# Two attention layers on one core: position rows in order of use, held weights, and the work at the seams of the second attention

## The chip, the core and the metric

The kernel runs on one core of one Trainium2 chip. The metric is the device time of one execution in microseconds. TensorE (PE) does the matmuls, VectorE (DVE), ScalarE (ACT) and GpSimd (POOL) work on what it leaves, and SyncE (SP) issues nearly all DMAs. All data are 32-bit floats.

## The reference

`x` has 8 batches of 32 x 32 positions (1024 tokens) and 512 channels. Each of two layers adds attention over the group-normalised input to its input:

```python
# layer 0: 16 heads of 32 channels
q, k, v = split(gn(x) @ w_qkv);  x = x + softmax(q * 32**-0.5 @ k.T) @ v @ w_proj + b_proj
# layer 1: 4 heads of 128 channels, with relative position logits
q = gn(x) @ Wq * 128**-0.5;  k = gn(x) @ Wk;  v = gn(x) @ Wv
scores = q @ k.T + rel_w[..., None, :] + rel_h[..., :, None]   # from q with pos_emb_w, pos_emb_h
x = x + softmax(scores) @ v @ Wo
```

## The kernel before

The batches are pipelined. In pass `b` of the outer loop, `attention_0` of batch `b` gives the beat, and `side_by_side` interleaves with it, by costs that each piece yields, the rest: the output projection WP of batch `b-1` (`after_0`), the output projection WO of batch `b-2` (`after_1`), the projections WQ1, WK1, WV1 of batch `b-1` (`second`), its `attention_1`, and the first projections of batch `b+1` (`before_0`). `total` is the expected sum of the costs (`PRODUCT` = 28 for one 512 x 512 projection, `SECOND` for `second`); the rest may advance while `done * steps < total * at`, with 65 steps. The steps of `attention_1` cost nothing, except in pass 7, so its 64 steps run as one block between two steps of `attention_0`. In pass 7 its first 32 steps are interleaved with `attention_0` of batch 7. Pass 8 has no `attention_0`, and after it `after_last` does the last WO projection. Below, batches are numbered 0 to 7, and "the opening of batch 2" is the start of its `attention_1`.

A projection is done with seven products of half-size blocks in place of eight, for each of two units (`seven`; `two_first` and `five_alone` in the last projection). A product takes one weight factor from `Stream`, and each product calls `stream.ahead()`, which loads the factor used seven products later. A factor of WV1 is two DMAs, kept for both units; the others are one. `forming` makes the four sums of the other operand that the seven products need (four DVE instructions, line L392). `woven(main, side, start, gap, places)` lets a side piece advance at certain steps of a main piece.

The second attention adds position logits to the scores. `position_logits` computes a short tile `pp` with matmuls and copies it to `pos` (L837, ACT) in four rounds, woven between the products of WK1 and WV1, each round followed by three yields. `Seeds` then writes `pos` to DRAM in two broadcast forms per head, `pc` and `pr` (L859), and reads back, in the 64 steps of the attention (4 heads, 2 halves of queries, 8 blocks of keys), one `columns` tile per 8 steps (L877) and one row tile per step (L880) into a ring of 8 in `pos`. POOL adds columns to rows (`add_up`, L887), and ACT copies the sum into a PSUM bank (`put`, L895). The score matmul accumulates onto that bank (L936), ACT takes exp (L938), the product with v is L949, and DVE adds up the exps (L963, L965). The copy of step `i` makes its ring slot free for the row of step `i+8`. At step `i`, copies are made up to step `i + AHEAD - 1` behind its exp; the four banks are those that `attention_0` used for its scores. `finish` ends each group of 8 steps: the sum is transposed and reduced on DVE (L688, L689), folded by a small matmul (L982), and the result divides q's columns on DVE (L703 to L720).

The order within each engine's queue is that of a planner, which runs through the program with its own costs and may put an instruction that is ready ahead of an earlier one that is not. `tc.issue_after(ins)` keeps the instructions of a block behind `ins` in its engine's queue.

Of the kernel before, what the change touches and what calls it, by code (L numbers as in the profile page):

```python
# [27 lines left out]
def quick_path(  # L28
# [23 lines left out]
    nc = tc.nc  # L52
# [4 lines left out]
    NT = N // P  # L57
# [136 lines left out]
    class Stream:  # L194
# [3 lines left out]
        def __init__(self, plan):  # L198
            self.plan = plan
            self.tiles = {}  # L200
            self.at = -1
            self.uses = iter([(n, i) for n, (_, _, _, some) in enumerate(plan) for i in some])
            for _ in ORDER:
                self.ahead()

        def load(self, n, i):
            m, rows, u, some = self.plan[n]
            if rows and u == 1 and not m.kept:
# [26 lines left out]

        def ahead(self):
            use = next(self.uses, None)
            if use is not None:
                self.load(*use)


# [298 lines left out]
    def in_two_parts(  # L540
        x, m, sinks, name, room=None, done=lambda u: None, behind=None, in_turn=False
    ):
# [32 lines left out]
        begin, rest = (3, five_alone) if in_turn else (2, five_last)  # L575
        yield from woven(products(), (next(sums) for _ in range(begin)), 0, 1)
        for u in range(2):
# [231 lines left out]
    def position_logits(q, turned, pos, b):  # L809
# [6 lines left out]
        for t in range(IW // (2 * G)):  # L816
# [24 lines left out]
            yield -2  # L841
            yield 0
            yield 0

    class Seeds:
# [4 lines left out]
        def __init__(self, pos, b):  # L850
            self.pos, self.b = pos, b
            self.kept = []
            for h in range(H1):
# [9 lines left out]
            self.rows, self.columns, self.summed = {}, {}, 0  # L863
            for i in range(self.ROWS):
                self.load(i)

        def load(self, i):
# [5 lines left out]
            if j == 0:  # L873
                to = self.columns[group] = mem.tile(
                    [P, NB], F32, tag="columns", name=f"columns_{self.b}_{group}", bufs=2
                )
                nc.sync.dma_start(to, by_columns)  # L877
            at = i % self.ROWS
            to = self.rows[i] = self.pos[:, at // NH, (at % NH) * NB : (at % NH + 1) * NB]
            nc.sync.dma_start(  # L880
                to, by_rows[16 * j : 16 * j + 16].unsqueeze(1).to_broadcast([16, P // 16, NB])
            )

        def add_up(self, upto):
# [13 lines left out]

    def attention_1(q, k, v, seeds, b, beside=0):

        steps = [(h, c, j) for h in range(H1) for c in range(NH) for j in range(NT)]
        state = {}
        AHEAD = 4
        scored = [None]
# [83 lines left out]
        for i, at in enumerate(steps):  # L988
# [13 lines left out]
            if i + 1 < beside:  # L1002
                prepare(i + 1)
            yield 0
        back(*pending)
        yield 0
        run(finish(*state.pop("ended")))
        state["pool"].__exit__(None, None, None)
# [166 lines left out]
    def second(b, st):  # L1175
# [19 lines left out]
        def queries(u):  # L1195
# [7 lines left out]
        keys_and_values = chain(  # L1203
            project_T(fs, WK1, k, f"k1_{b}"), project_rows(fs, WV1, v, f"v1_{b}")
        )
# [53 lines left out]
    def after_last(b, st):  # L1259
# [3 lines left out]
        sinks = [Onto(halves(xT, u), then=put_out(b, st, xT, u)) for u in range(2)]  # L1263
        run(in_two_parts(x, WO, sinks, f"wo_{b}", behind=(None, None, None, lambda: begun[0]), in_turn=True))

# [47 lines left out]
    PRODUCT = 2 * len(ORDER) * HC  # L1313
    SECOND = 3 * PRODUCT - 8

# [23 lines left out]

    states = [{} for _ in range(B)]  # L1340
    load_first(states[0])
    WV0.add_up([nc.gpsimd] * 2 + [nc.vector] * 2, nc.gpsimd, keep=True)
# [13 lines left out]

    def at_once(do):
        do()
        return
        yield  # L1360

    run(woven(before_first(states[0]), key_sums(), 3, 1))
    for b in range(B + 1):
# [5 lines left out]
        def forms_0(b=b, st=here):  # L1369
            st["ao0"] = forms(st["q0"], f"ao0_{b}")  # L1370

        def forms_past(b=b, st=past):
            forms_1(b - 2, st)

        if last is not None:
# [9 lines left out]
            else:  # L1385
                norm = norm_1(b - 1, last, after=lambda: summed[0], behind=lambda: begun[0])
            first = after_0(b - 1, last, forms_past if past is not None else None)
            rest.append(first if past is not None else with_norm(first))
            total += PRODUCT
# [3 lines left out]
            else:  # L1393
# [5 lines left out]
            attention = later(  # L1399
                lambda st, steps: attention_1(*st.pop("at"), steps), last, H1 * NT if shared else 0  # L1400
            )
# [520 lines left out]
```

## Time and profile before

| | |
|---|---|
| time, median of 3 runs | 3735.8 us (3732.56 to 3737.66) |
| profiled execution: time, span | 3736.12 us, 3734.3 us |
| mean granted TensorE clock | 0.992 |
| TensorE busy | 3659.2 us (98%) |
| DVE, ACT, POOL busy | 2562.3, 2032.8, 1300.5 us |
| DMA moved | 419.40 MB, mean 112 GB/s |
| row loads pos<-pr (L880) | 512 of 256 KB, median 4.3 us to landing |

The profile is of one execution. A line of a timeline gives start, length, engine, line of the program, operation, output and input, a count of merged instructions, and in brackets the idle time before it and what ended it. A line of the chain of waits gives who waited for whom, the sum, the number of times and the longest. SPq is SP's queue of DMA issues.

### The profile page before, as it was taken

To read this page: it belongs to the slowest core of one execution; us is meant where nothing else is said; L and a number is where in the kernel's file an instruction comes from. 1 tells how busy PE (TensorE), PEld (TensorE's weight loads), DVE (VectorE), ACT (ScalarE), POOL (GpSimd) and SP (SyncE) were. 2 spreads that over 40 slices of the span, in tenths; PEclk is the share of its full clock that TensorE was granted. 3 is DMA by queue.
4 is the path that set the end of the run, shared out by engine and by line. 5 is a ranking of instruction groups with operands and counts; after the bars stand their busy time and mean duration, and the time that the engine had idled before them with its cause. 6 is when DMAs were issued, how large, how long until landed. Compare 5 with 4: busy or idle time off the path is not lost.

```text
span 3734.3 us, 81210 instructions
## 1 busy us (share of the span) xinstructions
PE 3659.2 (98%) x33992; PEld 1251.2 (34%) x33998; DVE 2562.3 (69%) x2905; ACT 2032.8 (54%) x2281; POOL 1300.5 (35%) x847
## 2 busy tenths in 40 slices
PE   9999999999999999999999999999999999999998
PEld 4232243322433234332343323433234332333343
DVE  6778667685676856669576685766857668566545
ACT  3555655446554465544665446654566545655353
POOL 1342155131541315413163131721327112165254
PEclk9999999999999999999999999999999999999999
DMA  6122183233733337333372344713447133433385
GB/s 190 63 94 81 43 190 124 67 105 68 189 120 93 83 81 191 101 96 92 90 198 75 95 96 107 195 58 100 90 106 215 42 97 78 106 115 122 97 206 131
DMA packets 575158, 419.40 MB, mean 112 GB/s; under 512 B 279840, under 2 KB 471616, under 8 KB 573760
## 3 DMA queue, kind: packets, MB, share of 16 engines
q1 hardware_dynamic: 563152, 398.33, 39.9%
q0 software_dynamic: 2608, 13.70, 1.0%
q8 instruction: 270, 4.42, 0.5%
q10 hardware_dynamic: 9024, 2.10, 0.3%
q14 instruction: 104, 0.85, 0.1%
HBM read 321.72 MB, written 92.27 MB: 111 GB/s over the span
## 4 chain that ended last, share of the span: by engine, by line
PE 83%; DVE 7%; POOL 2%; ACT 2%; issue 2%; DMA 1%; SPq 1%; DVEq 0%; POOLq 0%; ACTq 0%
PE ps L739 13%; PE acc L765 11%; PE ps L936 11%; PE acc L949 11%; PE y_q L353 4%; PE y_v L353 4%; PE y_k L353 4%; PE z_q L353 3%; PE x_v L353 3%; PE z_v L353 3%; PE x_k L353 3%; DVE e_room L777 3%; PE z_k L353 2%; PE x_q L353 2%; PE y_wp L353 2%
## 5 line engine op out<-in xcount | busy, mean ns | idle before, releaser
L777 DVE TENSOR_TENSOR e_room<-e_room 128x2048 f32<-128x2048 f32 x448 | 1087.6, 2428 | 487.6 <-ACT e_room L754 485.7
L754 ACT ACTIVATE e_room<-ps 128x2048 f32<-128x2048 f32 x512 | 961.8, 1879 | 752.3 <-PE ps L739 717.4
L887 POOL TENSOR_TENSOR pos<-pos,columns 128x512 f32<-128x512 f32 x512 | 738.0, 1472 | 240.9 <-DMA pos<-pr 240.1
L739 PE MATMUL ps<-q,k 32*64 32x512 f32 x8192 | 592.6, 613 | 1.1 <-ACT e_room L754 1.0
L949 PE MATMUL acc<-e,v 128*128 128x512 f32 x1024 | 533.6, 605 | 27.6 <-ACT e L938 27.6
L765 PE MATMUL acc<-e_room,v 128*32 128x512 f32 x4096 | 551.1, 604 | 5.2 <-ACT e_room L754 5.2
L936 PE MATMUL ps<-q,k 128*128 128x512 f32 x1024 | 538.1, 610 | 9.5 <-ACT ps L895 9.5
L938 ACT ACTIVATE e<-ps 128x512 f32<-128x512 f32 x512 | 304.9, 597 | 261.9 <-PE ps L936 247.3
L965 DVE TENSOR_TENSOR es<-es,e 128x512 f32<-128x512 f32 x384 | 276.7, 721 | 155.8 <-ACT e L938 150.2
L895 ACT COPY ps<-pos 128x512 f32<-128x512 f32 x512 | 298.2, 590 | 92.3 <-POOL pos L887 49.7
L720 POOL TENSOR_TENSOR q<-q,su 128x512 f32<-128x512 f32 x64 | 94.8, 1481 | 568.0 <-DVE su L716 545.6
L949 PEld LDWEIGHTS acc<-e,v 128*128 128x128 f32 x1024 | 195.9, 193 | 283.2 <-issue 219.0
L936 PEld LDWEIGHTS ps<-q,k 128*128 128x128 f32 x1024 | 191.6, 194 | 248.6 <-issue 216.6
L739 PEld LDWEIGHTS ps<-q,k 32*64 32x64 f32 x8192 | 122.9, 129 | 395.6 <-issue 220.8
L765 PEld LDWEIGHTS acc<-e_room,v 128*32 128x32 f32 x4096 | 82.0, 108 | 420.6 <-issue 363.6
L605 POOL TENSOR_TENSOR k<-b_k,p_k 128x512 f32<-128x512 f32 x32 | 55.0, 1719 | 472.2 <-ACT p_k L457 461.5
L605 POOL TENSOR_TENSOR q<-b_q,p_q 128x512 f32<-128x512 f32 x32 | 67.3, 2102 | 356.9 <-ACT p_q L457 356.8
L605 POOL TENSOR_TENSOR v<-b_v,p_v 128x512 f32<-128x512 f32 x32 | 55.5, 1734 | 317.5 <-ACT p_v L457 306.2
L837 ACT COPY pos<-pp 32x512 f32<-32x512 f32 x128 | 104.1, 814 | 32.0 <-PE pp L828 30.8
L963 DVE TENSOR_TENSOR es<-e,e 128x512 f32<-128x512 f32 x64 | 66.2, 1035 | 56.2 <-ACT e L938 56.1
L681 DVE STREAM_TRANSPOSE tu<-su 128x512 f32<-128x512 f32 x64 | 45.2, 706 | 76.9 <-ACT su L679 76.7
L353 PE MATMUL y_q<-f_xn,w_q 128*32 128x512 f32 x768 | 91.4, 593 | 1.3 <-DVE a_q L443 0.6
(225 smaller groups left out, 4452.7 us busy)
## 6 DMA issues: line engine op xcount, KB each, us to landing
pos<-pr SPq DMA_DIRECT2D x512, 256.0 KB, 4.3
w_qkv<-ws_qkv SPq DMA_DIRECT2D x168, 128.0 KB, 2.6
d<-x0T SPq DMA_DIRECT2D x32, 512.0 KB, 5.8
x1T<-d SPq DMA_DIRECT2D x32, 512.0 KB, 5.4
d<-x1T SPq DMA_DIRECT2D x32, 512.0 KB, 3.5
pc<-pos SPq DMA_DIRECT2D x32, 512.0 KB, 8.2
pr<-pos SPq DMA_DIRECT2D x32, 512.0 KB, 9.0
columns<-pc SPq DMA_DIRECT2D x64, 256.0 KB, 4.2
```

What stands on the lines that cost most here:

```text
L353: ins = nc.tensor.matmul(out[columns, :], weights[:, columns], moving, start=start, stop=stop, skip_group_check=open_sum,)
L605: nc.gpsimd.tensor_tensor(self.dst[1][1], s(b), s(p7), op=ALU.add)
L739: nc.tensor.matmul(ps[some, r, :], k[m][rows, j * P + 64 * i : j * P + 64 * i + 64], q[m][rows, h * NB : (h + 1) * NB], start=True, stop=True,
L754: exps[0] = nc.scalar.activation(e, ps, AF.Exp, scale=D0 ** -0.5)
L765: nc.tensor.matmul(acc[r * D0 : (r + 1) * D0, :], v[:, j, c0 : c0 + D0], e[:, r, :], start=(j == blocks[0]), stop=(j == blocks[-1]),)
L777: summed[0] = nc.vector.tensor_add(state["esum"], state["esum"], e)
L887: nc.gpsimd.tensor_tensor(self.rows[i], self.rows[i], self.columns[i // NT], op=ALU.add)
L895: nc.scalar.copy(ps, rows)
L936: scored[0] = nc.tensor.matmul(ps, k[h][:, keys], q[:, h, queries], start=False, stop=True, skip_group_check=True)
L938: nc.scalar.activation(e, ps, AF.Exp, scale=1.0 / math.sqrt(D1))
L949: nc.tensor.matmul(acc, v[:, j, h * D1 : (h + 1) * D1], e, start=(j == 0), stop=(j == NT - 1),)
L965: added[0] = nc.vector.tensor_add(state["esum"], state["esum"], e)
```

## The change

Six edits are made together.

1. The loads of `Seeds` are chained with `issue_after` in the order of their use. The first two rows are loaded before the last head's position logits are written.
2. The weight loads of `Stream` stand behind the last load of `Seeds`. Those called by the second unit of WV1 are held and released one per step from step 6 of `attention_1` on.
3. `AHEAD` is 3 for 4: a bank's copy is made two steps ahead.
4. `SECOND` is one less.
5. In the last batch, `position_logits` yields twice per round for three times. In pass 7 the four sums of q for WP are spread over steps 45, 46, 53 and 54 of `attention_1`, not made at once at step 40.
6. In passes 7 and 8 the fold and the division of the last group of `attention_1` (L982, L703 to L720) are not run at its end, but after the second product of the projection that follows.

```diff
 class Stream:
+            self.held, self.waiting = False, 0
+            self.behind = None
         def load(self, n, i):
+            with tc.issue_after(self.behind.ins) if self.behind is not None else nullcontext():
+                self.fetch(n, i)
         def ahead(self):
+            if self.held:
+                self.waiting += 1
+                return
             use = next(self.uses, None)
...
+        def hold(self):
+            self.held = True
+            return
+            yield
+        def release(self):
+            if self.waiting:
+                self.waiting -= 1
+                self.held = False
+                self.ahead()
+                self.held = self.waiting > 0
...
 def in_two_parts(..., first=None):
-        yield from woven(products(), (next(sums) for _ in range(begin)), 0, 1)
+        ahead = chain(first or (), (next(sums) for _ in range(begin)))
+        yield from woven(products(), ahead, 0, 1)
...
 def position_logits(q, turned, pos, b):
-            yield 0
-            yield 0
+            for _ in range(1 if b == B - 1 else 2):
+                yield 0
...
 class Seeds:
+                if h == H1 - 2:
+                    self.load(0)
+                    self.load(1)
-            for i in range(self.ROWS):
+            for i in range(2, self.ROWS):
                 self.load(i)
...
-                nc.sync.dma_start(to, by_columns)
+                self.bring(to, by_columns)
...
+        def bring(self, to, rows):
+            with tc.issue_after(self.last.ins) if self.last is not None else nullcontext():
+                self.last = stream.behind = nc.sync.dma_start(to, rows)
...
-    def attention_1(q, k, v, seeds, b, beside=0):
+    def attention_1(q, k, v, seeds, b, beside=0, ends=None):
-        AHEAD = 4
+        AHEAD = 3
...
+            if i > 5:
+                stream.release()
             yield 0
-        run(finish(*state.pop("ended")))
+        last = finish(*state.pop("ended"))
+        if ends is None:
+            run(last)
+        else:
+            for _ in range(2):
+                next(last)
+            ends.append(0 for _ in last)
...
-            project_T(fs, WK1, k, f"k1_{b}"), project_rows(fs, WV1, v, f"v1_{b}")
+            project_T(fs, WK1, k, f"k1_{b}"),
+            project_rows(fs, WV1, v, f"v1_{b}", units=(0,)),
+            stream.hold(),
+            project_rows(fs, WV1, v, f"v1_{b}", units=(1,)),
...
-    SECOND = 3 * PRODUCT - 8
+    SECOND = 3 * PRODUCT - 8 - 1
...
+            if ends:
+                first = woven(first, ends.pop(), 0, 1)
...
-                    at_once(forms_0),
-                    H1 * NT + NT,
-                    H1 * NH * NT,
+                    forms_0_apart(),
+                    H1 * NT + NT + 5,
+                    NT,
+                    (0, 1),
```

More of the change, by code (lines that the diff above doesn't have):

```diff
@@ L206, in load, with fetch @@
         def load(self, n, i):
+            with tc.issue_after(self.behind.ins) if self.behind is not None else nullcontext():
+                self.fetch(n, i)
+        def fetch(self, n, i):
             m, rows, u, some = self.plan[n]
@@ L540, in in_two_parts @@
     def in_two_parts(
-        x, m, sinks, name, room=None, done=lambda u: None, behind=None, in_turn=False
+        x, m, sinks, name, room=None, done=lambda u: None, behind=None, in_turn=False, first=None
     ):
@@ L852, in __init__ @@
             self.kept = []
+            self.rows, self.columns, self.summed = {}, {}, 0
+            self.last = None
             for h in range(H1):
@@ L862, in __init__ @@
                 )
-            self.rows, self.columns, self.summed = {}, {}, 0
-            for i in range(self.ROWS):
+                if h == H1 - 2:
+                    self.load(0)
+                    self.load(1)
+            for i in range(2, self.ROWS):
                 self.load(i)
@@ L876, in load @@
                 )
-                nc.sync.dma_start(to, by_columns)
+                self.bring(to, by_columns)
             at = i % self.ROWS
             to = self.rows[i] = self.pos[:, at // NH, (at % NH) * NB : (at % NH + 1) * NB]
-            nc.sync.dma_start(
+            self.bring(
                 to, by_rows[16 * j : 16 * j + 16].unsqueeze(1).to_broadcast([16, P // 16, NB])
             )
+        def bring(self, to, rows):
+            with tc.issue_after(self.last.ins) if self.last is not None else nullcontext():
+                self.last = stream.behind = nc.sync.dma_start(to, rows)
         def add_up(self, upto):
@@ L1263, in after_last @@
         sinks = [Onto(halves(xT, u), then=put_out(b, st, xT, u)) for u in range(2)]
-        run(in_two_parts(x, WO, sinks, f"wo_{b}", behind=(None, None, None, lambda: begun[0]), in_turn=True))
+        run(
+            in_two_parts(
+                x, WO, sinks, f"wo_{b}", behind=(None, None, None, lambda: begun[0]), in_turn=True,
+                first=ends.pop(),
+            )
+        )
     def woven(main, side, start, gap, places=(0,)):
@@ L1340, in quick_path @@
     states = [{} for _ in range(B)]
+    ends = []
     load_first(states[0])
@@ L1355, in other_sums @@
             yield 0
[L1357 to L1360, printed above, removed]
     run(woven(before_first(states[0]), key_sums(), 3, 1))
@@ L1370, in forms_0, with forms_0_apart @@
             st["ao0"] = forms(st["q0"], f"ao0_{b}")
+        def forms_0_apart(b=b, st=here):
+            st["ao0"] = yield from forming(st["q0"], f"ao0_{b}")
         def forms_past(b=b, st=past):
@@ L1399, in quick_path @@
             attention = later(
-                lambda st, steps: attention_1(*st.pop("at"), steps), last, H1 * NT if shared else 0
+                lambda st, steps: attention_1(
+                    *st.pop("at"), steps, ends if coming is None else None
+                ),
+                last,
+                H1 * NT if shared else 0,
             )
```

## The prediction

> **What bounds the kernel now.** I read the page's busy shares first, then TensorE's waits, then one opening of the second attention as a timeline and in stretches, then the last batch.
>
> ```profile
> PE 3659.2 (98%) x33992; PEld 1251.2 (34%) x33998; DVE 2562.3 (69%) x2905; ACT 2032.8 (54%) x2281; POOL 1300.5 (35%) x847
> ```
>
> ```profile
> PE acc L949 <- ACT e L938: 27.6, 8, 4.9
> PE ps L936 <- ACT ps L895: 9.5, 6, 5.6
> PE acc L765 <- ACT e_room L754: 5.2, 5, 1.0
> PE sums L982 <- DVE fw L689: 5.0, 3, 2.8
> ```
>
> TensorE is the bound, so only its idle time, 75 us of the span, and time at a low clock can be won. Nearly all of its waits lie where attention_1 opens or ends. Taken one by one (start: length), the openings of batches 0 to 5 stall at 518.53: 3.81, 982.83: 3.97, 1439.60: 4.28, 1896.79: 4.89, 2354.41: 4.29, 2811.56: 3.99, together 25.23 us. Batch 2, on SP's queue and then on all engines:
>
> ```profile
> 1416.33 15.41 SPq L877 DMA_DIRECT2D columns<-pc  x2
> 1431.83 0.39 SPq L224 DMA_DIRECT2D w_qkv<-in_L_conv_w_qkv  x1
> ...
> 1434.87 0.42 SPq L224 DMA_DIRECT2D w_qkv<-ws_qkv  x1
> 1435.38 1.49 SPq L266 DMA_DIRECT2D xs<-in_x  x3
> 1436.97 4.40 SPq L880 DMA_DIRECT2D pos<-pr  x7
> ```
>
> ```profile
> 1441.41 11.06 POOL L887 TENSOR_TENSOR pos<-pos,columns 128x512 f32<-128x512 f32 x9 [10.03 <-DMA pos<-pr]
> ...
> 1442.71 0.59 ACT L895 COPY ps<-pos 128x512 f32<-128x512 f32 x1 [5.91 <-POOL pos L887]
> 1443.23 0.59 ACT L938 ACTIVATE e<-ps 128x512 f32<-128x512 f32 x1
> ...
> 1443.88 2.07 PE L949 MATMUL acc<-e,v 128*128 128x512 f32 x2 [4.28 <-ACT e L938]
> ```
>
> The line at 1416.33 merges two columns transfers. The second is issued at 1431.41, once GpSimd has ended an add at 1431.38. Behind it stand seven weights and three xs loads, and only then row 8, whose slot ACT had freed with the first copy (started 1428.09). So row 8 is issued at 1436.97 instead of about 1428.7. POOL, ACT's copy, the exp queued behind that copy and TensorE wait in turn.
>
> ```profile
> 1429.00:1439.60 10.60, 10.60 (x25) 4.48 (x24) 7.24 (x8) 6.20 (x12) 2.38 (x2) 1.00 0.62 154
> 1439.60:1443.30 3.70, 0.00 (x0) 0.00 (x0) 0.00 (x0) 0.59 (x2) 1.89 (x2) 0.99 1.00 270
> 1443.30:1450.00 6.70, 6.12 (x7) 2.52 (x8) 2.33 (x5) 3.42 (x6) 6.70 (x7) 0.50 1.11 244
> 1450.00:1548.00 98.00, 98.00 (x240) 44.07 (x238) 78.67 (x127) 66.95 (x115) 69.67 (x52) 1.00 0.58 170
> ```
>
> Columns: length, then PE, PEld, DVE, ACT, POOL busy, PEclk, DMA share, GB/s. After the stall the clock is 0.50 for 6.7 us; from 1450 on TensorE never waits. Per step it spends 4 x 0.429 = 1.72 us.
>
> **Part by part.**
>
> *Rows in order of use, weights held.* Each columns and row load now follows the one before it, so the second columns stands behind row 15. The seven weights wait for steps 6 to 12, behind rows 16 and later; those of the following unit stand behind row 63. Row 8 at 1428.7 + 4.3 (median landing of pos<-pr) + 1.27 (POOL add) is ready at 1434.3; the copy of row 8 follows exp 6, at about 1430.2 + 6 x 1.72 = 1440.5. Cover: 6 us. The 25.23 us go. The clock goes with them: half speed at 521.63-528.46, 985.84-992.67, 1443.23-1450.05, 1900.61-1907.44, 2358.00-2364.83, 2815.38-2818.80; from TensorE's restart in each, half of 6.1, 5.9, 6.2, 5.8, 6.1, 3.3 us was lost: 16.6 us.
>
> The Trainium skill, "TensorE: Matmul & The Clock Gate", Part 1, gives half rate after an idle window of about 3.4 us. Here the 2.85 us stall of batch 6 at 3391.66 was also followed by 3.4 us at half clock (3395.65-3399.06). By the rule batch 6 has 2.85 us to win, by the trace 2.85 + 1.7. I take the trace. Gaps up to 2.12 us left no half clock, so a short remainder costs only itself.
>
> "DMA: Bandwidth & Descriptors", Rules for kernel authors, speaks against holding weights: issue a DMA early and wait late. By it the holding costs one weight landing per batch, 3.6 us here, 25 us over seven batches. By the trace it costs nothing: from step 12 to 64 there are 52 x 1.72 = 89 us before the first use, and the unit behind row 63, which follows copy 55, still has about 8 steps and seven products. That cover is real only where the edge catches no weight needed sooner; see the last batch.
>
> *Copies two steps ahead (AHEAD 3).* Same instructions. In the steady stretch exp starts at 1450.66, the copy runs 1451.35-1451.94; the score two steps on would start at 1453.04. Margin 1.1 us, 0.5 where the copy of acc (L968, 0.58) comes between. At the opening three copies instead of four stand before exp 0, but only two scores before the first L949: 0 to 0.3 us each. I charge 0.3 x 6 = -1.8. For later transients (1.79 at 575.55, 2.12 at 3285.10, 1.17 at 3653.56; 5.1 in all) one step more of patience, and rows 0 and 1 some 5 us earlier, may save 0 to 5.1; I take 1.5.
>
> *SECOND less 1.* Totals become 201 for 202 in batches 1 to 5. At the attention_0 step 42 the 14th product of WV1 is no longer due (130 x 65 = 8450 against 42 x 201 = 8442), so it falls after step 43's exp and covers the L765 wait: five gaps of 1.04 go. In batch 0 (187 for 188) the boundary crosses the other way and one appears. Net 4 x 1.04 = 4.2 us.
>
> *forms_0 spread.* In batch 6 the L392 forms at 3390.39 (2.27 us) delayed L689, L982 and es. At steps 45, 46, 53, 54 each adds about 2.2 us of DVE to steps with 0.7 of 1.72 used; the backlog of about 2.4 us stays within the e1 buffers' 3.8 us. 4.55 us go.
>
> *Last folds woven.* Batch 6: L982 waits 1.08 us at 3446.39; now two products run first. +1.08. Batch 7: the fold moves from 3698.13 to about 3700.5, and rc, transpose, product, and the forms at 3700.49 (1.22), 3701.75 (2.19) and 3703.86 (2.30) move with it. The second form then ends at 3706.3, and y_wo, at 3705.35 now, waits for it: 1.0 us later, up to 3.5 if the x2T adds and transposes (0.68 + 0.71) get in between. Ends +1.1 and -3.5; I take -1.5.
>
> *Last batch.* Position copies come every second product: per pair 3.3 us of L837 copies and about 0.6 of others on ACT, in 2 x 1.72 + 0.87 for the pp matmuls. They fit; up to 1 us of TensorE waits for a bank, like the 0.55 and 0.56 there now. The writes then start about 6 us sooner (3545.7 for 3551.73), with rows 0 and 1 before the last two writes. Alone this removes the stall of 5.56, a 0.56 at 3583.67 and 1.7 of half clock: 7.8 us. But the spread now comes after the 13th product of WK1, and the 14th calls for WV1's seventh factor, which must then stand behind row 7.
>
> ```profile
> 3541.95 2.92 SPq L220 DMA_DIRECT2D w_v<-ws_v  x2
> ...
> 3569.12 7.68 SPq L880 DMA_DIRECT2D pos<-pr  x8
> 3578.04 1.42 SPq L224 DMA_DIRECT2D w_o<-in_L_conv_Wo  x2
> ```
>
> Row 7 is issued at 3576.2, in the new order about 3570.5; the w_o behind it took 7.3 us to land, so w_v lands near 3578, and the product that needs it ran at 3560.49. In fixed order TensorE idles 17 us and starts at half clock (3.4): 13 worse than now. If the planner runs the second half's four products that lack nothing (6.9 us) and first scores in between, some 7 us are idle, as much as today. I take 0, with ends +7.8 and -13.
>
> Sum: 25.2 - 1.8 + 16.6 + 1.5 + 4.2 + 4.55 + 1.1 - 1.5 + 0 = 49.9 us. The profiled execution took 3736.12 (span 3734.3 and 1.8 around it), 0.3 above the median of 3735.8; 3736.1 - 49.9 = 3686.
>
> **The rivals.**
> *A. The openings stall on.* At 1439.6-1443.3 DMA moved 270 GB/s at a share of 1.00. Rows need 256 KB per 1.72 us = 153 GB/s, seven weights another 76, xs on top: near that rate. Against: 6 us of cover, and rows 8 to 15 come before the weights. If half of 25.2 + 16.6 stays: 3707.
> *B. The last batch waits in order.* For: the edge takes in every weight traced after the rows. Against: the planner moves ready work ahead elsewhere (a later step's L765 runs before attention_1's scores). 3686 + 13 = 3699.
> *C. Slower: the copy binds every step.* With AHEAD 3 each score depends on a copy made 1.1 us before. Were the chain exp, copy, score longer than that margin by 0.1 us, 512 steps cost 51 us and the gain is gone; from there it decides, and 0.2 gives 3736 - 50 + 102 = 3788. Against: ACT is busy 0.60 + 0.59 of 1.72 us.
> *D. It does not do what it says.* The planner still puts a waiting transfer ahead of row 8; only pacing, forms and folds remain (4.2 + 4.55 + 1.1 - 1.5), about 8 us: 3728.
>
> **How the numbers follow.** Likeliest case 0.62, A 0.15, B 0.15, C 0.04, D 0.04. The prediction is 3686. The likeliest case's unknowns (last batch up to +7.8, transients, tail) span 3673 to 3697. Adding B and most of A gives 3670 to 3708. What a measurement can tell from no change is 0.2%, 7.5 us. Faster 0.94, same 0.02 (D's edge), slower 0.04 (C).
>
> **What would show it.** Right: no stall over 1 us and no half clock after the openings of batches 0 to 5; columns in SP's order behind row 15; attention_1 about 111 to 112 us long in batches 1 to 5 (119 now); L765 waits gone but one. In the last batch: where the w_v of the seventh factor is issued, and whether the wait stands at z_v or at the first scores. In the tail: y_wo waiting for L392. Wrong: DMA waits of POOL before row 8, or short ACT waits in every step.

## The result, and the profile after

The changed kernel takes 3713.14 us, median of 4 runs (3710.87 to 3716.11), against 3736.73 of the kernel before on the same chip (4 runs, 3732.56 to 3740.61): ratio 0.9938, 95% interval 0.992 to 0.9955. It gains 23.6 us. The forecast was 50, with a range of 28 to 66: the sign was right and the size was not. The traced execution after is the slowest of its four (3716.11), so the spans of the two traces differ by 20.1.

Cut at the last product with v (L949 before, L982 after) of each batch's `attention_1`, 0.43 us after its start, the two traces show where it went. The forecast column is the prediction's sum, put to the same stages (openings, their half clock, the first L949 wait and the pacing in batches 0 to 5; forms in batch 6; its fold in batch 7). The transients, 1.5, have no place of their own. The last two columns are of experiments told below.

| stage, us | before | after | forecast | measured | chain alone | best |
|---|---|---|---|---|---|---|
| start to end of attention_1 of batch 0 | 630.2 | 632.4 | -5.5 | +2.2 | 625.1 | 624.9 |
| batches 1 to 5 | 2288.4 | 2253.3 | -38.8 | -35.1 | 2252.6 | 2244.7 |
| batch 6 | 527.6 | 534.4 | -4.6 | +6.8 | 524.2 | 519.6 |
| batch 7 | 250.7 | 253.4 | -1.1 | +2.8 | 250.4 | 247.1 |
| tail | 37.4 | 40.6 | +1.5 | +3.3 | 37.7 | 37.3 |
| span | 3734.3 | 3714.2 | -50 | -20.1 | 3690.0 | 3673.5 |

Only batches 1 to 5 gained. That they come near the forecast is in part luck: five new stalls of 1.84 us, told below, are in the 35.1, and without them it would be some 44. All other stages lost. The waits of TensorE after (who waited for whom: sum, times, longest):

```profile
PE acc L982 <- ACT e L971: 14.5, 8, 3.1
PE ps L969 <- ACT ps L928: 6.6, 14, 1.3
...
PE z_v L375 <- DMA w_v<-ws_v: 3.0, 1, 3.0
PE sums L1015 <- DVE fw L712: 2.7, 1, 2.7
PE y_q L375 <- DVE a_q L465: 2.4, 2, 2.1
...
PE y_wo L375 <- DVE f_wo L414: 2.2, 1, 2.2
```

The L982 wait for exp has halved (27.6 before), and the L788 wait is one of 1.0 (five before). The waits of z_v for a weight and of y_wo for its sum are new, y_q's was 0.6 before, and that of sums was 5.0 in three. But for 0.69 in batch 7, none of the 14.5 is at an opening. In batch 2, SP's queue now reads (start, length):

```profile
1404.94 0.59 SPq L915 DMA_DIRECT2D columns<-pc  x1
1419.92 5.15 SPq L915 DMA_DIRECT2D pos<-pr  x6
...
1428.04 0.58 SPq L915 DMA_DIRECT2D columns<-pc  x1
1428.79 0.52 SPq L915 DMA_DIRECT2D pos<-pr  x1
1429.39 0.54 SPq L230 DMA_DIRECT2D w_qkv<-in_L_conv_w_qkv  x1
```

The columns transfer that had waited in front of row 8 comes after row 15, and the first weight comes after that. TensorE runs through. What holds it instead comes some 60 us later. POOL's timeline of the same attention:

```profile
1456.67 10.52 POOL L920 TENSOR_TENSOR pos<-pos,columns 128x512 f32<-128x512 f32 x8 [4.20 <-DMA pos<-pr]
1473.69 0.12 POOL L298 MEMSET mv<- 128x32 f32 x1 [6.50 <-DVE turned L327]
1473.77 3.73 POOL L920 TENSOR_TENSOR pos<-pos,columns 128x512 f32<-128x512 f32 x3
1479.07 1.02 POOL L342 TENSOR_TENSOR rstd<-var,neg_half 128x4 f32<-128x4 f32 x1 [1.57 <-DVE var L338]
1480.06 10.41 POOL L920 TENSOR_TENSOR pos<-pos,columns 128x512 f32<-128x512 f32 x7
```

A memset of 0.12 us, for a normalisation of a later pass, stands among the adds and waits 6.5 us for DVE. Three adds on, `rstd` of the same normalisation waits 1.57 us for DVE and runs 1.02. The adds behind them are late, and so are ACT's copy, the exp behind it and TensorE:

```profile
1481.36 0.59 ACT L928 COPY ps<-pos 128x512 f32<-128x512 f32 x1 [2.71 <-POOL pos L920]
...
1482.36 0.60 ACT L971 ACTIVATE e<-ps 128x512 f32<-128x512 f32 x1
...
1483.02 1.12 PE L982 MATMUL acc<-e,v 128*128 128x512 f32 x2 [1.85 <-ACT e L971]
```

Such a stall of 1.84 us stands in each of batches 1 to 5, and one of 3.07 with 6.8 us of half clock behind it in batch 0. The same memset and its wait stood in POOL's queue before, in batch 0 behind 33 adds and in batch 2 behind 35, where TensorE did not stall:

```profile
569.50 0.12 POOL L276 MEMSET mv<- 128x32 f32 x1 [10.98 <-DVE turned L305]
```

```profile
1488.56 0.12 POOL L276 MEMSET mv<- 128x32 f32 x1 [6.44 <-DVE turned L305]
```

In batch 6 two things went wrong. At its start a score of `attention_0` waits 1.18 us for ACT, and 10 us later y_q, a product of a projection, waits 2.08 for DVE, with 3.4 us at half clock behind it: the pacing moved a step of `attention_0` in front of y_q. And the sums of q, which were to lie apart, still run as one block. DVE's timeline:

```profile
3358.70 2.28 DVE L414 TENSOR_TENSOR f_ao<-q 128x1024 f32<-128x1024 f32 x1 [2.38 <-POOL q L743]
3360.90 1.75 DVE L998 TENSOR_TENSOR es<-es,e 128x512 f32<-128x512 f32 x1
3362.58 1.75 DVE L996 TENSOR_TENSOR es<-e,e 128x512 f32<-128x512 f32 x1
3364.24 0.70 DVE L711 STREAM_TRANSPOSE tu<-es 128x512 f32<-128x512 f32 x1
3364.87 1.66 DVE L414 TENSOR_TENSOR f_ao<-f_ao,q 128x1024 f32<-128x1024 f32 x1
3366.45 0.67 DVE L712 TENSOR_REDUCE fw<-tu 128x16 f32<-128x512 f32 x1
```

They start as soon as POOL has finished q. The program asks for them later, but the planner put them in front. `fw` waits behind them, and the fold with it: TensorE stands 1.48 and 2.66 us and then has 6.8 us at half clock.

In batch 7 the weight is where the prediction feared it, SP first, then TensorE:

```profile
3537.14 7.16 SPq L915 DMA_DIRECT2D pos<-pr  x6
3544.34 1.06 SPq L226 DMA_DIRECT2D w_v<-ws_v  x2
```

```profile
3543.09 1.98 PE L969 MATMUL ps<-q,k 128*128 128x512 f32 x4 [1.25 <-ACT ps L928]
3545.99 1.12 PE L969 MATMUL ps<-q,k 128*128 128x512 f32 x2 [0.92 <-ACT ps L928]
3548.15 1.12 PE L969 MATMUL ps<-q,k 128*128 128x512 f32 x2 [1.03 <-ACT ps L928]
3552.27 4.07 PE L375 MATMUL z_v<-w_v,x1T 128*32 128x256 f32 x36 [3.00 <-DMA w_v<-ws_v]
```

The planner fills the time with products of the second half and with scores 0 to 3. The half clock behind it, 6.8 us as before, falls on 5.2 us of work where it was 3.3, which costs 0.9 more. In the tail, y_wo waits 2.24 us for the second L414 form, and z_wo 1.67 for ACT (0.85 before).

### The profile page after: what moved, and what is told of

Read it like the earlier page. It is cut to its first block, busy times and chain, and to the rows that moved or that the text cites. A ratio compares the mean times of both kernels' runs of the same rounds, so it can differ in the third digit from the quotient of the medians.

```text
span 3714.2 us, 81237 instructions
## 1 busy us (share of the span) xinstructions
PE 3654.9 (98%) x33998; PEld 1247.2 (34%) x33998; DVE 2565.8 (69%) x2905; ACT 2030.6 (55%) x2281; POOL 1291.6 (35%) x847
## 4 chain that ended last, share of the span: by engine, by line
PE 89%; DVE 5%; ACT 2%; DMA 2%; issue 1%; POOL 1%; SPq 1%; ACTq 0%; DVEq 0%; POOLq 0%
PE ps L762 14%; PE acc L788 13%; PE ps L969 10%; PE acc L982 10%; PE y_q L375 4%; PE y_k L375 4%; PE y_v L375 4%; PE z_q L375 3%; PE x_k L375 3%; PE x_q L375 3%; PE x_v L375 3%; PE z_k L375 3%; PE z_v L375 3%; PE y_wp L375 2%; PE y_wo L375 2%; PE x_wp L375 2%
## 5 line engine op out<-in xcount | busy, mean ns | idle before, releaser
L788 PE MATMUL acc<-e_room,v 128*32 128x512 f32 x4096 | 546.8, 604 | 1.0 <-ACT e_room L777 1.0
L982 PE MATMUL acc<-e,v 128*128 128x512 f32 x1024 | 527.1, 598 | 15.0 <-ACT e L971 14.5
L743 POOL TENSOR_TENSOR q<-q,su 128x512 f32<-128x512 f32 x64 | 104.6, 1634 | 528.8 <-DVE su L739 525.5
L982 PEld LDWEIGHTS acc<-e,v 128*128 128x128 f32 x1024 | 193.1, 191 | 269.9 <-issue 207.2
L788 PEld LDWEIGHTS acc<-e_room,v 128*32 128x32 f32 x4096 | 81.4, 108 | 412.2 <-issue 363.0
L996 DVE TENSOR_TENSOR es<-e,e 128x512 f32<-128x512 f32 x64 | 74.3, 1161 | 63.7 <-ACT e L971 63.7
```

The lines of the kernel that those rows point to most:

```text
L788: nc.tensor.matmul(acc[r * D0 : (r + 1) * D0, :], v[:, j, c0 : c0 + D0], e[:, r, :], start=(j == blocks[0]), stop=(j == blocks[-1]),)
L982: nc.tensor.matmul(acc, v[:, j, h * D1 : (h + 1) * D1], e, start=(j == 0), stop=(j == NT - 1),)
```

## The experiments

Eighteen kernels were run, each beside the kernel before, which took 3729 to 3743 us. Kernels of one round below share a chip; across rounds the ratio to the kernel before is the surer measure.

### First round: one cause at each place

**e1_mvdve.** The memset moves to DVE. The orders of TensorE, ACT and SP stay the same.

```diff
-            nc.gpsimd.memset(st["mv"], 0.0)
+            nc.vector.memset(st["mv"], 0.0)
```

> The changed kernel with one edit: the memset of the tile mv (L298, 0.12 us) is done by DVE, not by POOL. The orders of TensorE, ACT and SP stay what they are. It bears on the new TensorE stall in the middle of attention_1: 1.84 us in each of batches 1 to 5, 3.07 us in batch 0 with about 3 us of half clock behind it. Theory POOL: that memset stands in POOL's queue ahead of the adds of rows and waits 6.5 us for DVE to read the tile before; the adds fall behind, then stand behind rstd (1.57 + 1.02 us) as well. Without it the stalls go: 5 x 1.84 + 3.07 + 3 = 15 us, 3698. Rival SP: the rows come late because four d<-x0T stores (3.5 us of SP's queue, 2 MB) stand ahead of columns and rows; then POOL waits for pos<-pr at the same place, the stalls stay and the time is 3713.

Measured 3700.31 us (3695.31 to 3704.28), ratio 0.990 (0.9885 to 0.9915). The stalls of 1.84 and 3.07 are gone; 0.60 is left in batch 0, 0.85 in batch 4, and 1.46 stands some 20 us into `attention_1` of batches 4 and 5, from a cause that was not sought. The same stretch of POOL:

```profile
1459.70 5.43 POOL L920 TENSOR_TENSOR pos<-pos,columns 128x512 f32<-128x512 f32 x4 [0.64 <-DMA pos<-pr]
1469.83 1.02 POOL L342 TENSOR_TENSOR rstd<-var,neg_half 128x4 f32<-128x4 f32 x1 [4.70 <-DVE var L338]
```

The adds have run ahead by then, so that rstd's longer wait (4.70) costs nothing. One instruction of 0.12 us in the wrong queue had cost 12.8 us (14 by the ratios). SP's order, with the d stores of the rival, is the same in both kernels.

**e2_ahead4.** `AHEAD = 4` for 3, nothing else.

> The changed kernel with AHEAD 4 again. Theory POOL with patience: with AHEAD 3 each add is asked for one step (1.72 us) later, so POOL has one add less done when rstd takes its place in the queue; with 4 the 1.84 us stalls of batches 1 to 5 go and batch 0 goes back to about 1.8: some 10 to 12 us, against up to 0.3 us more at each of six openings: 3701 to 3704. Rival: the stall was hidden before by the opening's own stall, which let rows run ahead, and AHEAD has no part in it: the 1.84 us stalls stay, the time is 3713 (or 2 more, by the openings).

Measured 3727.39 us (3721.27 to 3732.23), ratio 0.9976 (0.9966 to 0.9985): 14 us above the changed kernel, which neither theory had. The stalls grew to 0.32, 1.38 and 2.49 us (2.78 in one) in each of batches 1 to 5. In POOL's order the memset and rstd now come after 32 and 34 adds; with AHEAD 3 it was 33 and 36. A new theory: what counts is this place.

**e3_pass7.** In pass 7 SECOND is not one less, and the sums of q are tied down.

```diff
-            total += SECOND
+            total += SECOND + (b == B - 1)
...
-            st["ao0"] = yield from forming(st["q0"], f"ao0_{b}")
+            st["ao0"] = yield from forming(st["q0"], f"ao0_{b}", behind=lambda: added[0])
```

> The changed kernel with two edits in pass 7, at different places of the trace: SECOND is not one less there, and each of the four sums of q for WP (L414) stands behind the latest sum of exps in DVE's queue, so that the planner cannot make them early. Theory: the first takes away the wait of y_q for DVE (2.08), the 1.18 before it and the half clock after it (about 1.7), 5 us; the second keeps 2.3 us of DVE at a time out of the way of the fold of the fifth group, so 1.48, 2.66 and the 6.8 us at half clock (3.4) go, 7.5 us: 3701. Rival: DVE is too full wherever the sums stand, the wait of the fold for DVE only moves to a later group: 3708.

Measured 3701.03 us (3698.16 to 3703.54), ratio 0.9905 (0.989 to 0.992), as the theory said. Batch 6 takes 519.6 us in place of 534.4. The sums are now where the edit meant them, and the fold no longer waits:

```profile
3361.91 0.72 DVE L711 STREAM_TRANSPOSE tu<-es 128x512 f32<-128x512 f32 x1
3362.66 0.69 DVE L712 TENSOR_REDUCE fw<-tu 128x16 f32<-128x512 f32 x1
3372.12 1.21 DVE L414 TENSOR_TENSOR f_ao<-q 128x1024 f32<-128x1024 f32 x1
3373.86 1.68 DVE L414 TENSOR_TENSOR f_ao<-f_ao,q 128x1024 f32<-128x1024 f32 x1
```

**e4_last.** Two parts undone: three yields per round in the last batch, and the last fold of batch 7 at once.

```diff
-            for _ in range(1 if b == B - 1 else 2):
+            for _ in range(2):
...
-                    *st.pop("at"), steps, ends if coming is None else None
+                    *st.pop("at"), steps, ends if coming is None and here is not None else None
...
-                first=ends.pop(),
+                first=None,
```

> The changed kernel with two parts undone, at different places: in the last batch three yields per round of position copies, as before (so the seventh factor of WV1 is asked for before the rows and not held behind row 7), and the fold of the last group of batch 7 at the end of its attention, as before. Theory: at the opening of batch 7 the five gaps (1.25, 0.92, 1.03, 3.00, 0.69) and about 3 us of half clock go, since columns and rows now come in order with no w_o between: 10 us; the tail gives back its 3 to 4: 3700. Rival: the writes start some 6 us later and the first rows are then too late for the first scores, so that 3 to 5 us and a half clock stand there instead and only the tail is gained: 3709.

Measured 3704.47 us (3696.4 to 3705.05), ratio 0.9909 (0.9894 to 0.9924). Batch 7 takes 246.8 us for 253.4 and the tail 37.7 for 40.6. The theory holds but for 4 us: 1.57 and 1.81 remain at that opening, and 1.47 stands 20 us into `attention_1` of batch 3.

### Second round: do they add up, and what of the main part did it?

**e6_all.** The edits of e1, e3 and e4 together.

> The edits of three earlier runs together: the memset of mv on DVE; in pass 7 SECOND not one less and the four sums of q behind the sums of exps; in the last batch three yields per round, and the last fold of batch 7 at the end of its attention. Each acts at another place of the trace. If what was missing from the forecast is these three places, the savings add up by the medians: 3713.1 - 12.8 - 12.1 - 8.6 = 3680, and no half clock is left between 50 us and the last batch. Rival: they share causes (the planner's order shifts when one of them changes), and a good part is lost again: 3690 or more.

Measured 3676.68 us (3674.85 to 3680.1), ratio 0.9843 (0.9829 to 0.9856). They add up. Between 60 us and the tail no half clock is left.

**e7_mv_ahead4.** e1 and `AHEAD = 4`.

> The memset of mv on DVE, and AHEAD 4 for 3. With AHEAD 4 alone the time was 3727, 14 us above the changed kernel, with stalls of 1.4 and 2.5 us in each of batches 1 to 5, and the memset stood after 32 adds in place of 33. Theory order: only the memset's place in POOL's queue made these stalls; without it AHEAD is worth nothing but 0.3 us at an opening: 3700 to 3703. Rival patience: with four banks filled ahead a late row stops ACT one step sooner, whatever made it late (rstd stays in POOL's queue, 2 to 2.6 us), and 1 to 2.5 us stand in each batch: 3708 to 3714.

Measured 3709.32 us (3707.5 to 3714.72), ratio 0.9931 (0.9918 to 0.9945). The rival's number, but not yet its reason: 0.32 and 2.1 us stand in each of batches 1 to 5, and rstd comes after 34 adds where e1 has it after 36. Order and AHEAD are still mixed here.

**e8_weights.** e1, with the weights neither held nor behind the rows.

```diff
-            with tc.issue_after(self.behind.ins) if self.behind is not None else nullcontext():
+            with nullcontext():
                 self.fetch(n, i)
...
-            stream.hold(),
```

> The memset of mv on DVE, and weights neither held nor behind the rows; the rows stay chained. In SP's order 13 weights then stand between row 7 and row 8 of an opening, 5 ahead of the second columns and 8 behind it. Theory: it is the weights ahead of row 8 that stalled the openings, and the chain of rows alone does not help: at least the 25 us of stall and 17 of half clock of the kernel before come back, 3700 + 42 = 3742, more if 13 transfers cost more than the 7 of before. Rival: the second columns, which waited for GpSimd, was the cause, and with it in order the weights go by beside: 3700 to 3705.

Measured 3702.65 us (3695.89 to 3710.4), ratio 0.9914 (0.9899 to 0.9929): the theory, that the weights in front of row 8 were the stall, fell. No opening of batches 0 to 6 stalls in this trace. What it loses to e1 is 2.14 us in the middle of each batch, where rstd comes after 34 adds; what it wins is batch 7 (244.5 us for 252.8), whose w_v is no longer held.

**e9_rows.** e1, with the loads of `Seeds` not chained.

```diff
-            with tc.issue_after(self.last.ins) if self.last is not None else nullcontext():
+            with nullcontext():
                 self.last = stream.behind = nc.sync.dma_start(to, rows)
```

> The memset of mv on DVE, and the columns and row loads not chained; weights held and behind the last row called, as in the changed kernel. In SP's order the third columns then stands ahead of rows 8 to 13 and waits for the add of row 7. Theory: the weights were the cause of the stalls, and row 8 is late by some 3 us only, within the 6 us of cover: 3700 to 3703. Rival: a columns transfer that waits in SP's queue holds every row behind it and is enough for a stall of 2 to 4 us at each opening and half clock behind it: 3715 to 3730.

Measured 3736.73 us (3733.54 to 3741.28), ratio 1.0003 (0.9994 to 1.0011): the whole gain of e1, 36 us, is gone, more than the rival gave. SP and TensorE in batch 2:

```profile
1403.00 22.32 SPq L915 DMA_DIRECT2D columns<-pc  x2
1425.43 4.00 SPq L915 DMA_DIRECT2D pos<-pr  x6
```

```profile
1431.43 1.12 PE L982 MATMUL acc<-e,v 128*128 128x512 f32 x2 [2.42 <-ACT e L971]
```

With no weight near, the second of two columns transfers waits in SP's queue till 1425, when POOL has ended the adds that use its tile, and six rows wait behind it. The openings of batches 1 to 5 stall 2.4 to 3.0 us, 13.3 together, and that of batch 0 does not. In the middle of these batches 2.1 to 3.1 us stand as well, another 14 with waits of 0.32, and there rstd comes after 34 adds: by the trace about half of the loss is POOL's queue and not the openings.

### Third round: the chain alone, and POOL's queue made free

For e10 to e12, rstd stays on POOL, but is asked for four adds later:

```diff
-        nc.gpsimd.tensor_tensor(rstd, var, neg_half, op=ALU.pow)
+        def root():
+            with tc.issue_after(summer[0].ins) if summer[0] is not None else nullcontext():
+                nc.gpsimd.tensor_tensor(rstd, var, neg_half, op=ALU.pow)
+        if behind is None and after is None and out is None and summer[0] is not None:
+            queued.append([LATER, root])
+        else:
+            root()
...
+    summer, queued, LATER = [None], [], 4
...
+                if queued:
+                    queued[0][0] -= 1
+                    if not queued[0][0]:
+                        queued.pop()[1]()
```

The last lines stand in `add_up`, behind each add.

**e10_rstd** (with AHEAD 3) and **e11_rstd_ahead4** (with AHEAD 4), both with the memset on DVE.

> The changed kernel with the memset of mv on DVE and, in attention_1, rstd (L342) kept in POOL's queue behind four more adds than were asked for when it was called: it then stands after 38 adds, not 36. With the memset alone the time was 3700, with 0.6 us left in batch 0 and 0.85 in one other batch. Theory POOL: nothing over 0.4 us is left in the middle of attention_1, 3698 to 3700. Rival: the later rstd makes the normalisation of the next batch late, and the first products after attention_1 wait for the sums of xn: 3702 or more.

> The same with AHEAD 4. With the memset on DVE and AHEAD 4, rstd stood after 34 adds and not after 36, 0.3 and 2.1 us stood in each of batches 1 to 5, and the time was 3709. Here rstd stands after 39 adds. Theory order: AHEAD only moves the planner's place for what blocks POOL, and the stalls go: 3698 to 3702, no more than 2 above the same kernel with AHEAD 3. Rival patience: a bank filled one step earlier stops ACT one step earlier for any late row; 0.5 to 2 us stay in each batch, 3705 to 3710.

Measured 3692.43 us (3691.49 to 3694.13), ratio 0.9887, and 3697.78 us (3695.4 to 3699.28), ratio 0.9901. With rstd after 38 or 39 adds the stalls of batches 1 to 5 are gone with both, but for what is told below; these five batches take 2244.0 and 2243.6 us. The 5 us between them lie in batch 6 (527.9 and 532.9), where 0.41 and 1.60 us stand at the fold in one and 1.47 and 2.66 in the other. e10 gained 6 us more than its theory. In two batches waits of 1.1 and 0.3 remain in e10, and 0.32 in each in e11, but batch 6 of e10 is 7 us shorter than in e1, again at the fold (1.51 and 2.66 there, with 6.8 us at half clock).

**e13_bef_chain.** The kernel before, with nothing but the chain of rows.

```diff
+            self.last = None
...
-                nc.sync.dma_start(to, by_columns)
+                self.bring(to, by_columns)
...
-            nc.sync.dma_start(
+            self.bring(
...
+        def bring(self, to, rows):
+            with tc.issue_after(self.last.ins) if self.last is not None else nullcontext():
+                self.last = nc.sync.dma_start(to, rows)
```

> The kernel before with one part of the change: columns and rows are loaded each behind the one before. AHEAD 4, weights as before, in SP's order seven weights and xs stand ahead of row 8 but the third columns stands behind row 15. Theory chain: the 25 us of stall and 17 us of half clock at the openings go with this alone; the memset stands after 34 adds and rstd after 37 in POOL's queue, so 2 to 4 us come in the middle of five batches, 15 us: 3737 - 42 + 15 = 3710. Rival: without the hold the weights keep row 8 late: 3730 to 3737.

Measured 3692.76 us (3690.67 to 3694.54), ratio 0.9887 (0.9871 to 0.9904). This one part gains 42.3 us, near the 41.8 forecast for openings and their clock (by the traces 40.9 in batches 0 to 5, and 3.4 in batch 6 that were not forecast), and is 20 us faster than all six parts together. The 15 us feared for the middle did not come. Its SP queue has weights in front of row 8, but none of them waits there long, and the rows go on time:

```profile
1404.14 0.34 SPq L887 DMA_DIRECT2D columns<-pc  x1
1405.08 0.37 SPq L224 DMA_DIRECT2D w_qkv<-in_L_conv_w_qkv  x1
...
1412.56 0.42 SPq L224 DMA_DIRECT2D w_qkv<-in_L_conv_w_qkv  x1
1415.04 1.40 SPq L266 DMA_DIRECT2D xs<-in_x  x3
1416.58 3.30 SPq L887 DMA_DIRECT2D pos<-pr  x5
```

**e12_best.** Rows chained, weights free, memset and rstd as in e10, pass 7 as in e3, the last fold at once.

> What the runs so far point to, together: rows chained, weights neither held nor behind the rows, the memset of mv on DVE and rstd behind four more adds, pass 7 with SECOND not one less and the sums of q behind the sums of exps, position copies of the last batch every second product as in the changed kernel, the last fold of batch 7 at the end of its attention. Theory: free weights save in the last batch (gaps 0.73, 0.36, 0.70 at its opening, against 0.57, 0.52, 0.37, 1.84 in the best so far, 3676.7) and cost nothing elsewhere: about 3673. Rival: with the weights free the queue of SP is full when the rows of the last batch are asked for, or POOL's order shifts: 3678 or more.

Measured 3683.94 us (3673.93 to 3691.84), ratio 0.987 (0.9851 to 0.9889). The traced execution of 3673.9 is what the theory said, but two of the four are 16 to 18 us above it. So it is no better than e6, and its scatter was put to a test.

### Fourth round: which edit did it, and what holding is worth

**e14_ch_s9.** e13 with `SECOND` one less.

> The kernel before with two parts of the change: columns and rows chained, and SECOND one less. With the chain alone the time was 3692.8; the memset and rstd stood after 34 and 37 adds in POOL's queue in batches 1 to 5, and no stall came there. With SECOND one less the planner's order has them after 32 and 34 adds, and after 35 and 38 in batch 0. Theory: pacing is what brought the mid-attention stalls: 2.5 to 4.2 us in each of batches 1 to 5, 12 to 21 us, and 5 more in pass 7, against four gaps of 1.04 and 3.3 us in batch 0 won: 3702 to 3711. Rival: the stalls need AHEAD 3 or the hold, and SECOND gives its 4.2 us: 3688.

Measured 3725.25 us (3719.85 to 3733.0), ratio 0.9978 (0.997 to 0.9986). One count less in the pacing costs 32 us on top of the chain (34 by the ratios), 14 more than the theory's worst case. POOL's order now has the memset after 32 adds, and TensorE stands twice in each of batches 1 to 5:

```profile
1471.67 0.12 POOL L276 MEMSET mv<- 128x32 f32 x1 [14.76 <-DVE turned L305]
1471.76 2.48 POOL L892 TENSOR_TENSOR pos<-pos,columns 128x512 f32<-128x512 f32 x2
1475.58 1.02 POOL L320 TENSOR_TENSOR rstd<-var,neg_half 128x4 f32<-128x4 f32 x1 [1.33 <-DVE var L316]
```

```profile
1473.70 1.12 PE L941 MATMUL ps<-q,k 128*128 128x512 f32 x2 [0.78 <-ACT ps L900]
...
1479.03 1.13 PE L954 MATMUL acc<-e,v 128*128 128x512 f32 x2 [2.49 <-ACT e L943]
```

Each pair is followed by 3.4 us at half clock, and batch 6 takes 538.5 us for 524.2 (waits of 1.18 and 2.08 us that e13 hasn't, and of 3.59 and 2.66 where it has 2.13 and 1.02).

**e15_ch_a3.** e13 with `AHEAD = 3`.

> The kernel before with columns and rows chained, and AHEAD 3. The memset and rstd stand after 34 and 37 adds as with the chain alone (3692.8). Theory order: with POOL's order the same, AHEAD is worth next to nothing: 3690 to 3695. Rival: two steps ahead leave ACT too little patience, or one step less to stand in for a late row: stalls of 0.5 to 2 us in batches 1 to 5, or the transients of batch 0 and of the last batch shorter by as much: outside that range.

Measured 3695.99 us (3692.8 to 3698.84), ratio 0.9902 (0.9887 to 0.9917). The intervals of the two overlap; batches 1 to 5 take the same time to 0.1 us, and in batch 0 one step less ahead is 1.4 us longer. It is 1 us above the theory's range, but AHEAD is worth nothing that these runs can tell.

**e16_best2** and **e17_best2_free**: e6 with rstd as in e10; and that with the weights free.

> The best so far (3676.7: memset on DVE, SECOND not one less in pass 7, sums of q behind the sums of exps, three yields per round in the last batch, last fold of batch 7 at the end of its attention) with rstd behind four more adds as well; weights held. In that kernel 0.60, 0.56, 1.23 and 0.49 us stood at attention_1 of batches 0, 1, 3 and 4. Theory: these go, 3 us: 3674. Rival: they are no more than scatter of DMA landings that rstd has no part in: 3677.

> The same with the weights neither held nor behind the rows. The two kernels that had free weights spread over 14 and 18 us between runs, the others over 3 to 9. Theory: the hold is idle on average: within 2 us of the kernel with held weights, and as steady. Rival: weights ahead of row 8 use up the cover of the rows in some runs, so that an opening stalls with its half clock: a median 3 to 12 us above, and a spread of over 10 us.

Measured 3673.84 us (3672.41 to 3676.87), ratio 0.9841 (0.9827 to 0.9854), and 3678.95 us (3675.91 to 3680.54), ratio 0.9851 (0.9836 to 0.9866). e16 is the fastest kernel of the study, 60 us under the kernel before and 39 under the changed one (36 by the ratios). Its waits:

```profile
PE turned L1118 <- DMA x_rows<-in_x: 4.9, 1, 4.9
PE ps L983 <- ACT ps L942: 4.9, 12, 2.3
PE acc L996 <- ACT e L985: 3.4, 3, 1.6
PE x_v L385 <- issue: 3.4, 1, 3.4
```

The two longest single waits, 4.9 and 3.4, are at the start of the program. In the middle 1.59 and 0.48 us remain in batches 3 and 4, and there the first round's rival may have its part. POOL in batch 3:

```profile
1926.97 9.52 POOL L930 TENSOR_TENSOR pos<-pos,columns 128x512 f32<-128x512 f32 x7 [2.70 <-DMA pos<-pr]
```

These rows stand behind the four d stores in SP's queue; no run moved the stores, so their part is not shown. With free weights the time is 5 us longer here, not within the 2 of the theory: stalls of 1.16 and 1.44 some 20 us into two batches, and 0.32 in each of batches 1 to 5. The intervals overlap, and the spread was 5 us and not over 10; what made e12 scatter stays open.

### Fifth round

**e18_pace.** e16 with `SECOND` not one less in any pass. **e19_bef_chain_pool.** e13 with the memset and rstd as in e10.

> The best version (3673.8) with SECOND not one less in any pass; POOL's order is the same (no memset, rstd after 38 adds). Theory: the pacing by itself is worth the four gaps of 1.04 us forecast for it, and its cost came from POOL's queue: 3673.8 + 4.2 = 3678, with five waits of 1.04 us for e_room and none in batch 0. Rival: a product at another place shifts other engines' order too, and it is more than 3 us away from that, either side.

> The kernel before with columns and rows chained, the memset of mv on DVE, and rstd behind four more adds (after 39 of them); nothing else of the change. With the chain alone the time was 3692.8, with 0.78 and 2.50 us in batch 0 and nothing in the middle of batches 1 to 5. Theory: batch 0 gains its 3.3 us and nothing else changes: 3689 to 3690. Rival: the later rstd or DVE's memset shifts other work: 3693 or more.

Measured 3686.41 us (3685.72 to 3688.0), ratio 0.9862 (0.9843 to 0.988), and 3688.55 us (3686.09 to 3689.66), ratio 0.9867 (0.9848 to 0.9886). e19 is as expected: batch 0 loses its 3.3. e18 is not, and its rival held: with POOL out of it, pacing is worth 8 us by the ratios, whose intervals just overlap, more than 4.2. By its trace each of batches 1 to 5 is 2 to 5 us longer than in e16, of which 1.04 is the wait for e_room and 0.32 one in attention_1; the rest lies in pieces too small to be listed. Batch 0 is 2.2 shorter.

The kernels put side by side by POOL's order, batches 1 to 5:

| kernel | adds before memset, rstd | stalls in the middle of attention_1, us |
|---|---|---|
| before | 35, 38 | none |
| e13 (chain alone), e15 | 34, 37 | none |
| after | 33, 36 | 1.84 |
| e14 | 32, 34 | 0.78, 2.49 |
| e2 | 32, 34 | 0.32, 1.38, 2.49 |
| e7, e8, e9 | on DVE, 34 | 0.32, 2.1 (3.1 and 2.8 in two batches of e9) |
| e1, e6 | on DVE, 36 | 0.85 in one batch of e1; 0.56, 1.23, 0.49 in three of e6 |
| e10 to e12, e16 to e19 | on DVE, 38 or 39 | 0.33 at most in 30 batches of 35; else 1.1 (e10), 1.59 and 0.48 (e16), 0.47 (e17), 0.92 (e18) |

Batch 0 fits: 33, 35 gave 1.79 before; 32, 35 gave 3.07 after; 35, 38 in e14 gave none. What the last two rows keep is scattered over the batches of one trace, with the same order in all.

## Why the prediction was wrong, point by point

*Rows in order of use, weights held (41.8 with the clock).* Right in sum and in mechanism, wrong in which half does it. The chain alone gives 42.3 (e13); without it openings stall again, though 13.3 us in all and not 25.2 (e9). The prediction read seven weights between the late columns and row 8 as part of the delay; they were there because the columns held them up as well. With 13 weights in front of row 8, e8 and e13 have no stall at these openings. Holding them was costed at nothing for the openings and proved to gain 0 to 5 us (e16 against e17), but the held w_v of batch 7 cost 8 (e1 against e8). By the rule of the Trainium skill, "DMA: Bandwidth & Descriptors", Rules for kernel authors, to issue a DMA early and wait late, the prediction's estimate for holding was a cost of 25 us: in batches 0 to 6 the trace was the better guide, as the prediction chose; in batch 7 holding did cost, as the rule would have it.

*Copies two steps ahead (-1.8, +1.5 for transients).* The term was about right taken alone (e15: no difference that can be told). What failed is the assumption behind the transients: that they could only shrink. They were read as lack of patience in the banks. The one of batch 0 was POOL's queue: with the chain it is 2.50 at AHEAD 4 (e13) and 3.27 at AHEAD 3 (e15), and it goes when POOL's queue is freed (e19). What makes the other two is not shown. The prediction saw batch 0's 1.79 us at 575.55 and did not ask what POOL was waiting for there, though in batches 1 to 5 the same memset stood in the same queue, two adds further on and out of harm.

*SECOND less 1 (+4.2).* This step failed most. The five gaps of 1.04 went and one appeared, to the letter. But the planner orders every queue anew, and a product moved by one step moved the memset and rstd forward among POOL's adds: -32 us on the chain alone (e14), of which 21 in batches 1 to 5 and 14 in batch 6, less 1.3 won in batch 0 (by the traces). In batches 1 to 5 the loss came by that queue: with POOL free, the same edit gains 8 us (e16 against e18). In the changed kernel the other edits softened it: 12.8 us by e1, and of the 12.1 of e3 the part at y_q (1.18, 2.08 and half a window of half clock). The prediction costed the edit on TensorE's schedule alone.

*forms_0 spread (+4.55).* Failed: the sums were not spread. The prediction took the program's steps 45 to 54 for the time of execution, although it had itself noted that the planner moves ready work ahead, and used that in another part. Tied behind the sums of exps they are spread, and batch 6 is then 8.1 us under before (e3); but 3.4 of these come with the chain alone (e13), and a transient of 2.12 has gone too, so what the spread alone is worth was not measured.

*Last folds woven (+1.1, -1.5).* Batch 6's wait of 1.08 is gone. The tail lost 3.3, inside the 1 to 3.5 given.

*Last batch (0, between +7.8 and -13).* The mechanism was seen: w_v behind row 7, the planner's filling, some 7 us idle. Gaps of 1.25, 0.92, 1.03, 3.00 and 0.69 make 6.9, close to the 6.1 of before. The stage came out 2.8 longer: by the trace 0.9 is half clock, the idle time is the same, and the other 1.9 lie in the same number of matmuls, for a reason that is not shown. With three yields it is 6.6 shorter (e4).

*The rivals.* None had the mechanism. A's 3707 was nearest to 3713.1, by luck: it put the loss at the openings, which were won. The planner was treated as something that might undo an edit, not as something that lets an edit of one engine reorder another.

The chain alone at 3692.8, and the best version at 3673.8, say that 3686 was within reach of a version of the change. What e1, e3 and e4 took away one by one was 12.8 (POOL), 12.1 (pass 7) and 8.7 us (last batch and tail), 33.6 of the 36.5 between the changed kernel and e6.

## What to carry to other kernels

Where a planner orders the queues, list for each queue the instructions that wait for another engine, however short they are, and count what stands behind them: an edit of pacing elsewhere can move them by one place. A stall that shows in one batch alone, like the 1.79 us of batch 0, is worth asking for its cause: the same queue stands in the others, a few instructions away. Tie down what must be late; program order alone does not do it.

## What was not expected of the hardware

The prediction noted that gaps up to 2.12 us had left no half clock, and one of 2.85 had. Over these traces the same gap did either: y_q's 2.08 us was followed by 3.4 us at half clock in the changed kernel and in e1, and by none in e4 and e7. In the records of the granted clock all half-clock stretches of a trace begin on one grid of 3.413 us. The table puts the stretch from 60 to 3650 us of all 20 traces on that grid and sorts the windows at full speed by the time that TensorE was idle in them, as the trace models it; the limits were drawn from these same traces.

| idle in the window, us | windows | followed by a window at half clock |
|---|---|---|
| 0.5 to 1.5 | 290 | 0 |
| 1.5 to 1.95 | 37 | 5 |
| 1.95 or more | 51 | 51 |

The Trainium skill, "TensorE: Matmul & The Clock Gate", Part 1, describes a free-running window of this length, and the grid agrees. It speaks of an idle window; here a window four sevenths idle is enough. So by these counts a stall under 1.5 us, alone in its window, costs only itself; one over 3.9 puts 1.95 into some window wherever it falls, and brings half clock always; one of a size between does or doesn't by its place on the grid. A window at half clock is worth up to 1.7 us. That executions of one kernel scatter by this is likely but not shown, since each kernel has one trace.
